# Starting block 1's loop over groups during block 0's last periods, in SBUF that earlier stages have left

## The chip, the core and the metric

The kernel runs on one core of one Trainium2 chip. A core has five engines that run side by side: TensorE (matrix products), VectorE, ScalarE, GpSimd, and SyncE, which here only starts transfers. Each engine takes its instructions in order. The metric is device microseconds of one execution. The median before the change is 1409.62 us over three runs (1408.16 to 1410.97).

## What is computed

Two blocks work on 8192 tokens (32 sequences of 256) of width 128, all in float32. Cut to what matters here:

```python
# block 0
xn = layernorm(x)
s  = attention_and_mlp(xn)            # two layers: norm, softmax attention, norm, MLP of 512
m0 = routed0(xn) + shared0(xn)        # 64 experts, each takes the first 64 tokens that chose it
x  = x + s * silu(m0)
# block 1
xn = layernorm(x)
s  = linear_attention(xn)             # keys and values twice, product of states, norm
top = argmax(xn @ gate_w)             # one of 32 experts for each token
xs  = xn * sigmoid(max(xn @ gate_w))
g  = silu(shared1(xn) + expert[top](xs))
out = x + s * g
```

For block 1 the tokens are sorted by expert: a token's place is the start of its expert plus its rank, the number of earlier tokens that chose the same expert.

## The kernel before, in words

The tokens form 64 tiles of 128, and 16 groups of four tiles; two groups are a pair. The Tile framework decides the order of each engine's queue when the program is built: it follows the order of the calls, lets a later instruction pass one that it takes to be waiting, and adds the semaphore waits. A tile comes from a pool, under a tag with a number of buffers ("bufs"); a new tile waits until the old one in its buffer is no longer used. Pools that are closed give their SBUF to later pools, with the same kind of wait.

**Block 0** (L135 to L594) runs in 18 periods, the loop over `k` at the end of its scope. `order_of` lists 16 units, each a pair and a layer. Period k interleaves, step by step, the softmax of unit k (`softmax`, L393), the second norm, MLP and projections of its neighbours (`beside`, L539), the choice of block 0's experts (`front`, `search`, `share`, in periods 0 to 6) and two groups of four experts (`experts(q)`, L297). An expert group gathers tokens with GpSimd (L305), and adds its results into the DRAM tensors `moe0[0]` and `moe0[1]` by indirect DMA (L343). They run in periods 8 to 15. Periods 16 and 17 hold only the end of the MLP: `narrow` (L496, matmuls L500) reads weights that lie in the pool w0.

**Block 1** begins behind that. Its pools w1 and wk1 are opened when block 0's are closed, so they lie where block 0's were. Each group g passes `route(g)` and then `shared1(g)`:

1. L635 to L642: load the two parts of m0 (tiles c_g and c_m), add them on GpSimd (L638), load x, apply silu on ScalarE, multiply by s_rows (which is s) and add to x, both on VectorE.
2. `normed` (L104): statistics on VectorE (L110, L111), the root by a power on GpSimd (L112, L113), and with `on_act=False` the scaling of four tiles on GpSimd (L121) into c_xn.
3. Four transpositions on TensorE (L128), a copy by ScalarE (L648).
4. The router's matmuls (L652), maximum and index on VectorE (L660, L661), the one-hot `hot` (L664), the score (L666).
5. s_rows is set to xn times the score (L670, ScalarE). GpSimd adds up `before`, the counts of earlier tiles (L673, L678), TensorE turns them into ranks (L676, L677), and VectorE stores `rank` (L681).
6. to 8. The shared expert: two halves (L690 to L693) and the second product (L698), stored by L704.

`rolling(steps, 2)` (L719) starts a new group after every second round over the groups that are under way, one step of each a round. Each of these steps ends at a `yield`, and a group's end is a step too, so that 16 groups make 144.

When all ranks are known, the places `dest` follow (L738 to L768), then 64 indirect DMAs send the rows to `xslot` (`send`, L774), `linear_attention` (L787) runs for 15 groups beside it, `routed` (L863) runs the experts in 24 lots of four tiles, and `finish` (L915) writes the output.

Of the kernel before, what the change touches and what calls it, by code (L numbers as in the profile page):

```python
# [25 lines left out]
P = 128  # L26
# [3 lines left out]
GT = 4  # L30
# [30 lines left out]
def recurrent_kernel(ctx: ExitStack, tc: tile.TileContext, x, consts, small0, wsd, wgu, wd, small1, bias1, wr, out):  # L61
# [35 lines left out]
    zero = keep.tile([P, GT * (D + 1)], F32, name="zero")  # L97
    pool.memset(zero, 0.0)
# [5 lines left out]
    def normed(wk, src, dst, on_act=False):  # L104
# [9 lines left out]
        if on_act:  # L114
            ins = pool.tensor_tensor(rs[:, 1], mv[:, :, 0], rs[:, 0], ALU.mult)
            for j in range(GT):
                vec.tensor_scalar(dst[:, j], src[:, j], rs[:, 0, j : j + 1], rs[:, 1, j : j + 1], ALU.mult, ALU.subtract)
            return ins
        pool.tensor_scalar(rs[:, 1], mv[:, :, 0], -1.0, 0.0, ALU.mult, ALU.add)
        for j in range(GT):  # L120
            ins = pool.tensor_scalar(dst[:, j], src[:, j], rs[:, 1, j : j + 1], rs[:, 0, j : j + 1], ALU.add, ALU.mult)  # L121
# [12 lines left out]

    with ExitStack() as c0:  # L135
        w0 = c0.enter_context(tc.tile_pool(name="w0", bufs=1))
        wk = c0.enter_context(tc.tile_pool(name="wk0", bufs=2))
# [4 lines left out]
        def fetch(g):  # L142
            xi = wk.tile([P, GT, D], F32, name="x_in", bufs=3)
            sp.dma_start(xi, rows(x, g))
            return xi
# [34 lines left out]
        iot = w0.tile([P, GW], F32, name="iot")  # L180
        for h in range(2):
            pool.iota(iot[h * E0 : (h + 1) * E0], [[-1, GW]], base=T - h * GW, channel_multiplier=0, allow_small_or_imprecise_dtypes=True)
        ciota = w0.tile([E0, C0], F32, name="ciota")
        pool.iota(ciota, [[1, C0]], base=0, channel_multiplier=0, allow_small_or_imprecise_dtypes=True)
        cand = w0.tile([P, NG // 4, C0], F32, name="cand")
        keys, lent, found = {}, {}, []

        def enter(g):
# [7 lines left out]
            xt = wk.tile([P, GW], F32, name="xs", bufs=5)  # L196
# [4 lines left out]
        def choose(p):  # L201

            sel = wk.tile([P, GT, 2, E0], F32, name="sel")
            for h in range(2):
# [6 lines left out]
                nm = wk.tile([P, GT], F32, name="r_nm")  # L211
                vec.tensor_reduce(nm, lg3, AX.X, ALU.max, negate=True)
                ex = wk.tile([P, GT, E0], F32, name="r_ex")
                rep = wk.tile([P, GT, E0], F32, name="r_rep")
                m8 = wk.tile([P, GT, K0], F32, name="r_m8")
# [7 lines left out]
                su = wk.tile([P, GT], F32, name="r_su")  # L223
# [4 lines left out]
                wt = wk.tile([P, GT, E0], F32, name="r_wt")  # L228
# [7 lines left out]
            if p % 2 == 0:  # L236
                keys[p // 2] = wk.tile([P, 2 * GW], F32, name="key", bufs=2)
# [35 lines left out]
        def places():  # L273
            top = w0.tile([P, C0], F32, name="top")
            yield from largest(top, cand.rearrange("p q c -> p (q c)"))
            both = w0.tile([E0, 2 * C0], F32, name="both")
# [4 lines left out]
            first = w0.tile([E0, C0], F32, name="first")  # L281
            yield from largest(first, both)

            slot = w0.tile([E0, 2, C0], F32, name="slot")
# [83 lines left out]
        def project(g, l, got):  # L368
# [6 lines left out]
            for i, rot in enumerate(("rotq", "rotk")):  # L375
                ps = bank()
                pe.matmul(ps, w[i], xt, start=True, stop=True)
                t = wk.tile([P, GW], F32, name=f"a_qk{i}", bufs=4)
# [9 lines left out]
            v = wk.tile([P, GT, D], F32, name="a_v", bufs=4)  # L388
# [4 lines left out]
        def softmax(gs, l, qkv, early):  # L393
# [3 lines left out]
            def scores(g, b):  # L397
# [11 lines left out]
                nm = wk.tile([P, 4], F32, name="a_nm", bufs=4)  # L409
# [4 lines left out]
            def exp(g, b, sc, nm):  # L414
                pr = wk.tile([P, 4, SEQ], F32, name="a_pr", bufs=3)
                su = wk.tile([P, 4], F32, name="a_su", bufs=4)
# [15 lines left out]
            def turn(g, b, pr):  # L432
                pt = wk.tile([P, 2, HEADS, SEQ], F32, name="a_pt", bufs=2)
# [7 lines left out]
            def mix(g, b, pt):  # L441
# [8 lines left out]
                if b == 0:  # L450
                    at[g] = wk.tile([P, GW], F32, name="a_at")
# [136 lines left out]

        for k in range(units + 2):
            steps = [beside(k), front(k), search(k), share(k)]  # L590
            steps += [experts(q) for q in range(E0 // 4) if min(8 + q // 2, 15) == k]
            if k < units:
                gs, l = unit(k)
                steps = [softmax(gs, l, qkv, k < 7), *steps]  # L594
            drain(run(*steps))
# [4 lines left out]
    s1, n_s1 = columns(SMALL1)  # L600
    sw1 = w1p.tile([P, n_s1], F32, name="sw1")
    sp.dma_start(sw1, small1)
    bias = w1p.tile([P, 5 * D], F32, name="bias1")
    sp.dma_start(bias, bias1.broadcast_to([P, 5 * D]))

    def par1(name, at=0, n=None):
        a, b = s1[name]
        return sw1[:, a + at : b if n is None else a + at + n]

# [4 lines left out]

    xt_all = w1p.tile([P, T], F32, name="xt_all")
    x_all = w1p.tile([P, NT, D], F32, name="x_all")
    hot = w1p.tile([P, NT, E1], F32, name="hot")
    rank = w1p.tile([P, NT], F32, name="rank")
    before = w1p.tile([P, GT + 1, E1], F32, name="before")
    vec.memset(before, 0.0)  # L620
    ones = w1p.tile([P, P], F32, name="ones")
    vec.memset(ones, 1.0)
    eiota = w1p.tile([P, E1], F32, name="eiota")
    pool.iota(eiota, [[1, E1]], base=0, channel_multiplier=0, allow_small_or_imprecise_dtypes=True)
# [6 lines left out]
    def route(g):  # L631

        tl = slice(g * GT, (g + 1) * GT)
        gr = wk.tile([P, GT, D], F32, tag="gate", name="c_g", bufs=3)
        sp.dma_start(gr, rows(moe0[0], g))  # L635
        more = wk.tile([P, GT, D], F32, tag="chan", name="c_m", bufs=3)
        sp.dma_start(more, rows(moe0[1], g))
        pool.tensor_tensor(gr, gr, more, ALU.add)  # L638
        sp.dma_start(x_all[:, tl], rows(x, g))
        act.activation(gr, gr, AF.Silu)  # L640
        vec.tensor_tensor(gr, gr, s_all[:, tl], ALU.mult)
        vec.tensor_tensor(x_all[:, tl], x_all[:, tl], gr, ALU.add)  # L642
        yield
        xn = wk.tile([P, GT, D], F32, tag="tok", name="c_xn", bufs=3)
        normed(wk, x_all[:, tl], xn)
        yield
        ps = transposed(xn)
        act.copy(xt_all[:, g * GW : (g + 1) * GW], ps)  # L648
        yield
        lp = bank()  # L650
        for j in range(GT):
            pe.matmul(  # L652
                lp[:, j * E1 : (j + 1) * E1], xt_all[:, (g * GT + j) * P : (g * GT + j + 1) * P], par1("router"),
                start=True, stop=True,
            )
        lg = lp[:, : GT * E1].rearrange("p (t e) -> p t e", e=E1)
        m8 = wk.tile([P, GT, 8], F32, name="c_m8")
        i8 = wk.tile([P, GT, 8], U32, name="c_i8")
        for j in range(GT):
            vec.max(m8[:, j], lg[:, j])  # L660
            vec.max_index(i8[:, j], m8[:, j], lg[:, j])  # L661
        fi = wk.tile([P, GT], F32, name="c_fi")
        vec.tensor_copy(fi, i8[:, :, 0])
        vec.tensor_tensor(hot[:, tl], bcast(eiota, 1, GT), bcast(fi, 2, E1), ALU.is_equal)  # L664
        score = wk.tile([P, GT], F32, name="c_sc")
        act.activation(score, m8[:, :, 0], AF.Tanh, scale=0.5)  # L666
        yield
        vec.tensor_scalar(score, score, 0.5, 0.5, ALU.mult, ALU.add)
        for j in range(GT):
            act.activation(s_all[:, g * GT + j], xn[:, j], AF.Copy, scale=score[:, j : j + 1])  # L670

        for j in range(GT):
            pool.tensor_tensor(before[:, j + 1], before[:, j], hot[:, g * GT + j], ALU.add)  # L673
        ps = bank()
        ranks = ps[:, : GT * E1]
# [39 lines left out]
    def drain(i):  # L715
        for _ in i:
            pass
# [313 lines left out]
```

## Time and profile before

| | us |
|---|---|
| Median of three runs | 1409.62 |
| The profiled execution, its own time | 1416.91 |
| Its span, first to last instruction | 1415.1 |
| TensorE busy | 1245.2 (88%) |
| VectorE busy | 926.6 (65%) |
| ScalarE busy | 771.6 (55%) |
| GpSimd busy | 703.4 (50%) |
| Mean granted TensorE clock | 0.953 |

All times in the trace count from the start of the span. Block 0 ends at 808 us, the loop over groups at 984, the sends at about 1105. An engine is called busy while one of its instructions runs; matmuls overlap, so a group of them is shorter than the sum of its durations. DVE is VectorE, ACT ScalarE, POOL GpSimd, PE TensorE and PEld its weight loads. The granted clock is the share of full speed at which TensorE ran. A line such as "A <- B" in a list of waits says that A's engine stood idle until B was done.

### The profile page before, as it was taken

The numbers are of one execution on the slowest core, as the hardware profiler recorded it, in microseconds if no ns is written. First come the engines' busy times: TensorE is split into PE (matmuls) and PEld (weight loads), VectorE is DVE, ScalarE is ACT, GpSimd is POOL, SyncE is SP. The second block draws the span as 40 slices with busy tenths as digits, with TensorE's granted clock in tenths as the row PEclk, the third lists the DMA queues.
The fourth block names the chain that finished last, engine by engine and source line by source line (L and its number), as shares of the span: only waits on it lengthen the run. The fifth ranks groups of instructions, "written<-read, shape, count | busy, mean of one in ns | idle before, by whom it ended". The sixth has DMA issues, their size and how long they took to land. (4 is left out here: it accounts for less than half of the span.)

```text
span 1415.1 us, 22851 instructions
## 1 busy us (share of the span) xinstructions
PE 1245.2 (88%) x7395; PEld 872.8 (62%) x7395; DVE 926.6 (65%) x2971; ACT 771.6 (55%) x1842; POOL 703.4 (50%) x1116
## 2 busy tenths in 40 slices
PE   6988998899899999999999758899756899899897
PEld 4545665665567666776666525566434778787763
DVE  4689899869956676566655355746555565665437
ACT  1775566566756766766757333443423454555342
POOL 6353437352356666676574176642566444343440
PEclk9989999999999999999999968999778899999999
DMA  6021332310202212222211174211411466666666
GB/s 185 9 56 54 108 110 70 106 34 5 90 13 47 47 26 40 53 52 45 45 18 9 35 215 127 58 38 38 123 53 51 129 189 203 191 191 203 185 199 195
DMA packets 141783, 128.95 MB, mean 91 GB/s; under 512 B 17792, under 2 KB 117088, under 8 KB 141536
## 3 DMA queue, kind: packets, MB, share of 16 engines
q1 hardware_dynamic: 129888, 111.72, 26.8%
q0 software_dynamic: 11776, 15.78, 4.9%
q8 instruction: 59, 0.97, 0.3%
q14 instruction: 60, 0.49, 0.1%
HBM read 85.20 MB, written 42.25 MB: 90 GB/s over the span
## 5 line engine op out<-in xcount | busy, mean ns | idle before, releaser
L904 POOL DMA_INDIRECT back<-e_ys,e_toi x96 | 97.1, 1011 | 137.7 <-ACT e_ys L903 108.0
L420 ACT ACTIVATE a_pr<-ps_sc,a_nm 128x256 f32<-128x256 f32 x256 | 119.4, 479 | 74.6 <-DVE a_nm L411 63.7
L112 POOL TENSOR_SCALAR bn_rs<-bn_mv 128x4 f32<-128x4 f32 x112 | 26.9, 241 | 243.6 <-DVE bn_mv L111 228.7
L482 PE MATMUL ps_mm<-xt,sw 128*128 128x512 f32 x256 | 132.8, 622 | 2.8 <-ACT r_ex L217 2.0
L121 POOL TENSOR_SCALAR z<-s_rows,bn_rs 128x128 f32<-128x128 f32 x256 | 129.4, 517 | 6.9
L500 PE MATMUL ps_mm<-sw,m_h 128*128 128x128 f32 x1024 | 128.0, 281 | 2.7 <-ACT a_at L452 1.3
L500 PEld LDWEIGHTS ps_mm<-sw,m_h 128*128 128x128 f32 x1024 | 120.1, 194 | 15.3 <-issue 5.6
L343 POOL DMA_INDIRECT moe<-e_y,sidx x64 | 93.2, 1456 | 59.7 <-ACT e_y L339 44.1
L487 DVE SCALAR_TENSOR_TENSOR m_h<-m_h,m_z 128x512 f32<-128x512 f32 x128 | 89.1, 702 | 48.9 <-ACT m_h L486 48.3
L113 POOL TENSOR_TENSOR bn_rs<-bn_rs,power 128x4 f32<-128x4 f32 x112 | 114.7, 1024 | 1.3
L484 ACT ACTIVATE m_z<-ps_mm,fold 128x512 f32<-128x512 f32 x128 | 86.8, 687 | 43.4 <-PE ps_mm L482 43.2
L411 DVE TENSOR_REDUCE a_nm<-ps_sc 128x2 f32<-128x512 f32 x128 | 83.1, 682 | 31.4 <-PE ps_sc L405 29.3
L890 PE MATMUL ps_sc<-e_xt,e_w 128*128 128x128 f32 x768 | 100.5, 278 | 3.3 <-ACT e_xt L877 2.4
L890 PEld LDWEIGHTS ps_sc<-e_xt,e_w 128*128 128x128 f32 x768 | 93.8, 194 | 9.6 <-issue 5.6
L405 PE MATMUL ps_sc<-a_qk,a_qk 64*128 64x256 f32 x512 | 95.4, 412 | 1.4 <-ACT a_pr L420 1.2
L486 ACT ACTIVATE m_h<-m_z 128x512 f32<-128x512 f32 x128 | 80.3, 636 | 1.8
L437 PEld LDWEIGHTS ps_tr<-con,a_pr 128*128 128x128 f32 x512 | 58.8, 144 | 32.2 <-issue 20.3
L774 POOL DMA_INDIRECT xslot<-s_rows,dest x64 | 64.1, 1002 | 27.9 <-issue 17.9
L437 PE MATMUL ps_tr<-con,a_pr 128*128 128x128 f32 x512 | 74.6, 280 | 3.4 <-DVE key L238 2.4
L438 ACT COPY a_pt<-ps_tr 128x512 f32<-128x512 f32 x128 | 70.4, 590 | 10.1 <-PE ps_tr L437 8.9
L899 PE MATMUL ps_mm<-e_w,e_hs 128*128 128x128 f32 x384 | 61.7, 288 | 15.1 <-DVE e_hs L896 11.1
L446 PE MATMUL ps_mm<-a_pt,a_v 128*64 128x256 f32 x512 | 71.5, 398 | 3.5 <-ACT r_ex L217 2.2
(226 smaller groups left out, 2956.6 us busy)
## 6 DMA issues: line engine op xcount, KB each, us to landing
e_w<-in_wr_dram SPq DMA_DIRECT2D x96, 384.0 KB
xslot<-zero SPq DMA_DIRECT2D x4, 1548.0 KB
e_x<-xslot SPq DMA_DIRECT2D x24, 258.0 KB
e_wg<-in_wgu_dram SPq DMA_DIRECT2D x16, 384.0 KB
x_in<-in_x_dram SPq DMA_DIRECT2D x16, 256.0 KB
tab<-s_rows SPq DMA_DIRECT2D x16, 256.0 KB
moe<-s_y SPq DMA_DIRECT2D x16, 256.0 KB
moe<-zero SPq DMA_DIRECT2D x4, 1024.0 KB
```

The source lines that it names most:

```text
L113: pool.tensor_tensor(rs[:, 0], rs[:, 0], power, ALU.pow)
L121: ins = pool.tensor_scalar(dst[:, j], src[:, j], rs[:, 1, j : j + 1], rs[:, 0, j : j + 1], ALU.add, ALU.mult)
L343: pool.indirect_dma_start(out=moe0[e % 2], out_offset=bass.IndirectOffsetOnAxis(ap=sidx[:, 4 * q + e : 4 * q + e + 1], axis=0), in_=ye[:, ...
L405: pe.matmul(sc[h][:, j * SEQ : (j + 1) * SEQ], qk[0][hd, q0 : q0 + P], qk[1][hd, b * SEQ : (b + 1) * SEQ], start=True, stop=True,)
L420: act.activation(pr[:, n], sc[h][:, j * SEQ : (j + 1) * SEQ], AF.Exp, bias=nm[:, n : n + 1], accum_out=su[:, n : n + 1],)
L437: pe.transpose(pts[:, n * P : (n + 1) * P], pr[:, n, k * P : (k + 1) * P], ident)
L482: pe.matmul(ps, par("w1", l * FF0 + f * P, P), xt, start=True, stop=True)
L484: act.activation(z, ps, AF.Identity, bias=fold[:, l, 3 + f : 4 + f])
L487: vec.scalar_tensor_tensor(h, h, 1.0, z, ALU.add, ALU.mult)
L500: pe.matmul(ps[:, j * D : (j + 1) * D], hs[f][:, j * P : (j + 1) * P], par("w2", l * FF0 + f * D, D), start=f == 0, stop=f == 3,)
L890: pe.matmul(ps[:, c * P : (c + 1) * P], wt[:, c * P : (c + 1) * P], xt[:, j * P : (j + 1) * P], start=True, stop=True,)
L904: ins = pool.indirect_dma_start(out=back, out_offset=bass.IndirectOffsetOnAxis(ap=toi[:, j : j + 1], axis=0), in_=ys[:, j], in_offset=None,)
```

## The change

- Block 1's helpers (`route`, `shared1`, `rolling`, `begin`) are defined ahead of block 0. The iterator `begun` over the loop's steps is made ahead of the periods; 12, 30 and 20 of its steps are taken in periods 15, 16 and 17, and the rest is drained where the loop stood.
- Block 0's pools move to the other end of SBUF. Those of the token choice (wf) close before period 7, and those of attention (wa) before period 16. In the room that they leave, the pools first_work and first are opened before period 7 (groups 0 to 3, one buffer for each tag), and mid_work and mid before period 16 (groups 4 to 8, two buffers). Groups 9 to 15 keep their tiles in w1.
- x_all, xt_all and hot are split into tiles for each group or quarter. Where three buffers of a tag rotated, `work(n)` now takes first_work if n % 3 is 0, and mid_work otherwise; linear attention, the experts and `finish` use these too.
- Groups 0 to 7 use tanh for silu: silu(x) = 0.5 (1 + tanh(x/2)) x.
- Block 1's norm scales on ScalarE, and s_rows is scaled on GpSimd.
- GpSimd no longer counts. VectorE adds up the four tiles of a group (`c_cum`), TensorE makes of them the ranks and the group's count, and `before` holds a count for each group. The counts are then added in the dest stage by quarters.
- Block 0's experts run in periods 7 to 14.
- The weights small1 are loaded in two parts: router and shared expert (sw_c) in period 7, the rest (sw_a) at the old place.

```diff
-    def normed(wk, src, dst, on_act=False):
+    def normed(wk, src, dst, on=pool):
...
         pool.tensor_scalar(rs[:, 1], mv[:, :, 0], -1.0, 0.0, ALU.mult, ALU.add)
+        if on is act:
+            pool.tensor_tensor(rs[:, 1], rs[:, 1], rs[:, 0], ALU.mult)
+            for j in range(GT):
+                ins = act.activation(dst[:, j], src[:, j], AF.Identity, scale=rs[:, 0, j : j + 1], bias=rs[:, 1, j : j + 1])
+            return ins
...
+    EARLY, TANH = 4, 8
...
+    def room(pool_, gs):
+        for g in gs:
+            x_at[g] = pool_.tile([P, GT, D], F32, name=f"x_{g}")
+            xt_at[g] = pool_.tile([P, GW], F32, name=f"xt_{g}")
+            if g % 4 == 0:
+                hots[g // 4] = pool_.tile([P, NT // 4, E1], F32, name=f"hot_{g // 4}")
...
+    def work(n):
+
+        return works[len(works) > 1 and n % 3 > 0]
+
+    def route(g):
+
+        wk = works[0] if g < EARLY else work(g)
...
+        if g < TANH:
+
+            act.activation(more, gr, AF.Tanh, scale=0.5)
+            vec.scalar_tensor_tensor(gr, more, 1.0, gr, ALU.add, ALU.mult)
+            vec.scalar_tensor_tensor(gr, gr, 0.5, s_all[:, tl], ALU.mult, ALU.mult)
+        else:
+            act.activation(gr, gr, AF.Silu)
+            vec.tensor_tensor(gr, gr, s_all[:, tl], ALU.mult)
...
+        normed(wk, x_at[g], xn, act)
...
+        for j in range(GT):
+            pool.tensor_scalar(s_all[:, g * GT + j], xn[:, j], score[:, j : j + 1], 0.0, ALU.mult, ALU.add)
...
+        cum = wk.tile([P, GT, E1], F32, name="c_cum")
+        vec.tensor_copy(cum[:, 0], hot[:, 0])
+        for j in range(1, GT):
+            vec.tensor_tensor(cum[:, j], cum[:, j - 1], hot[:, j], ALU.add)
+        ps = bank()
+        pe.matmul(ps[:, : GT * E1], const("tri"), hot.rearrange("p t e -> p (t e)"), start=True, stop=False)
+        pe.matmul(
+            ps[:, E1 : GT * E1], at1["ones"], cum[:, : GT - 1].rearrange("p t e -> p (t e)"), start=False, stop=True,
+        )
+        pe.matmul(ps[:, GT * E1 : (GT + 1) * E1], at1["ones"], cum[:, GT - 1], start=True, stop=True)
+        vec.tensor_tensor(at1["before"][:, g + 1], at1["before"][:, g], ps[:, GT * E1 : (GT + 1) * E1], ALU.add)
...
+        begun = rolling([begin(g) for g in range(NG)], 2)
         for k in range(units + 2):
+            if k == 7:
+                cf.close()
+                works.append(ctx.enter_context(tc.tile_pool(name="first_work", bufs=1)))
+                begin1(ctx.enter_context(tc.tile_pool(name="first", bufs=1)))
+            if k == 16:
+                ca.close()
+                works.append(ctx.enter_context(tc.tile_pool(name="mid_work", bufs=2)))
+                room(ctx.enter_context(tc.tile_pool(name="mid", bufs=1)), range(EARLY, 9))
             steps = [beside(k), front(k), search(k), share(k)]
-            steps += [experts(q) for q in range(E0 // 4) if min(8 + q // 2, 15) == k]
+            steps += [experts(q) for q in range(E0 // 4) if 7 + q // 2 == k]
             if k < units:
                 gs, l = unit(k)
                 steps = [softmax(gs, l, qkv, k < 7), *steps]
+            more = {15: 12, 16: 30, 17: 20}.get(k)
+            if more:
+                steps.append(some(begun, more))
             drain(run(*steps))
...
-    drain(rolling([begin(g) for g in range(NG)], 2))
+    drain(begun)
...
-        vec.tensor_tensor(hot[:, tq], hot[:, tq], bcast(padf, 1, NT // nq), ALU.mult)
+        gq = slice(q * NG // nq, (q + 1) * NG // nq)
+        vec.tensor_tensor(before[:, gq], before[:, gq], bcast(padf, 1, NG // nq), ALU.add)
+        hq = hots[q].rearrange("p (g t) e -> p g t e", t=GT)
+        for j in range(GT):
+            vec.tensor_tensor(hq[:, :, j], hq[:, :, j], before[:, gq], ALU.mult)
```

## The prediction

> **What bounds the kernel now.** I read the page first (its 40 slices of 35.4 us), then busy time by stretch, then the waits and the chain inside the stretch that the change touches. Rows 2 of the page, TensorE's busy tenths and its granted clock:
>
> ```profile
> PE   6988998899899999999999758899756899899897
> ...
> PEclk9989999999999999999999968999778899999999
> ```
>
> TensorE is full from slice 6 to slice 22, falls to 7 and 5 just after it, recovers by slice 26 and dips again at 28. The first dip is the start of block 1's loop over groups. The windows (start:end, length, then busy us and instructions of PE, PEld, DVE, ACT, POOL; granted clock, DMA share, GB/s) give it numbers:
>
> ```profile
> 713.00:772.00 59.00, 56.13 (x364) 37.84 (x364) 35.16 (x100) 38.34 (x98) 38.56 (x50) 1.00 0.12 12
> 772.00:800.00 28.00, 25.00 (x113) 14.83 (x110) 11.25 (x23) 16.01 (x28) 3.80 (x8) 0.94 0.00 1
> 800.00:808.60 8.60, 7.33 (x64) 6.95 (x62) 2.77 (x4) 2.37 (x4) 0.42 (x3) 1.00 0.00 0
> 808.60:905.00 96.40, 62.34 (x248) 41.05 (x249) 55.12 (x249) 31.26 (x72) 64.47 (x117) 0.77 0.55 154
> 905.00:984.00 79.00, 74.90 (x407) 50.68 (x406) 44.49 (x230) 37.08 (x92) 32.73 (x93) 1.00 0.12 35
> 984.00:1106.00 122.00, 81.52 (x325) 54.75 (x323) 71.81 (x190) 44.80 (x50) 71.27 (x79) 0.76 0.24 73
> ```
>
> The first three rows are block 0's periods 15, 16 and 17; the fourth is the loop's ramp, the fifth its steady part. In periods 15 to 17 TensorE is the bound while the others are at 30 to 65%; in the ramp nothing is full. The chain of waits says why:
>
> ```profile
> 800.89 6.75 PE ps_mm L500 x58
> ...
> 811.38 7.54 DMA c_m<-moe
> 819.06 1.79 POOL c_g L638
> ...
> 825.07 0.97 POOL bn_rs L113
> 826.15 1.77 POOL c_xn L121 x4
> ...
> 941.88 1.79 PE ps_mm L698 x16
> ...
> 949.50 1.79 PE ps_mm L698 x16
> ```
>
> Nothing of block 1 begins before block 0's last matmul, because its tiles lie where block 0's lay. Then a load (7.5 us) and a chain over four engines come before the first transposition at 826.7. Later the chain repeats every 7.6 us (941.88 to 949.50), ending in L698: the steady pace of a group. The waits in 808 to 990 (total us, times, longest):
>
> ```profile
> PEld ps_tr L128 <- POOL c_xn L121: 30.0, 18, 19.2
> ...
> PEld ps_mm L676 <- POOL before L673: 21.5, 15, 5.3
> ...
> PEld ps_mm L652 <- ACT xt_all L648: 2.2, 1, 2.2
> ```
>
> One wait of 19 us, then many of 0.6 to 1.5 us on GpSimd: 64.5 of 96.4 us busy there.
>
> **TensorE's work, counted at full clock.** I add what TensorE must do from 713 (start of period 15) to 984 (the loop's end), 271 us.
> - Block 0: 56.13 + 25.00 + 7.33 = 88.5 us, less 1.4 us that were only a slower clock (780 to 790, granted 0.78 and 0.88): 87.1. At period 15's own fill (56.13/59 = 95%) this takes 91.6.
> - The loop: 16 groups at 7.6 us = 121.6. Check: busy times the clock over 5 us windows gives 50.9 for the ramp, plus 74.9, less about 5 of linear attention (L809) that already ran before 984: 121.
> - Of 271 us, 271 - 213.2 = 58 therefore go to idle, to the clock and to waits.
>
> Weighing the clock: the Trainium skill (TensorE: Matmul & The Clock Gate, section What's actually happening) says that the clock halves after an idle window of about 3.4 us and is whole again after one busy window. The loop has one such long gap, so by the rule 3.4 x 0.5 = 1.7 us are lost. The windows show more: 62.3 us busy in the ramp did 50.9 us of work, 11.4 lost, with 0.50 granted still at 865 to 870 where single waits are 2 to 5 us. By the rule the gain below would be 10 us less; I take the windows.
>
> **The change, part by part.**
> - *62 of the loop's 144 steps go into periods 15 to 17* (12, 30, 20; each group has eight steps and an end). With lag 2 that is groups 0 to 5 whole, five steps of 6, three of 7: about 55 us of TensorE work by the rows (per group 0.9 L128, 1.0 L652, 0.9 ranks, 2.2 per half of the shared expert, 1.8 L698). It is added to TensorE, not hidden there; what vanishes is the ramp. After: 213.2, plus what follows.
> - *Do the other engines hold it?* Vector: 49.2 us busy now in periods 15 to 17. A tanh group is 10.7 us by durations (3 x 0.70 gate, 1.75 statistics, 1.83 max and index, 0.51, score 0.27, counts 0.95, ranks 0.57, 4 x 0.68 shared); durations overlap, busy is 0.77 of their sum in 808 to 984, so 8.2. For 6.8 groups 56: 105 of about 145 us. Scalar: 56.7 + 6.8 x 5.2 = 92. GpSimd: 42.8, less two experts' 14, plus 6.8 x 4.9 = 62. None binds. The drained rest has silu groups at 8.6 x 0.77 = 6.6 Vector us against TensorE's 7.9: nearer, not over.
> - *Counts.* GpSimd loses 4 x 0.294 + 0.273 = 1.45 us a group. Vector gains a copy, three 128x32 adds and one add from PSUM, about 0.95 (0.19 each: between a 128x8 search, 0.19, and a 128x128 product, 0.29). TensorE gains one matmul of 32 columns: 0.3 (L742's pair) to 0.5 (two of L676), I take 0.3: 4.8 us in all, less 0.3 for L742 dropped. This is on the path: **+4.5**. What it buys is the 1.43 us wait on L673 (21.5/15).
> - *Normalising on Scalar, scaling s_rows on GpSimd.* A swap: 4 x 0.474 (L121) against 4 x 0.39 (L670), with a second pointer operand 0.09 more each (L852 776 ns against L484 687). Even; nothing queued behind them is the bound.
> - *Tanh for groups 0 to 7*: Vector +0.70 for the gate and +1.38 for f_h, inside the sum above. It keeps the exponential's table: a load is 1.28 us (L640), and only one stays.
> - *Experts in 7 to 14*: gathers ran at 392.5, right after gidx (389.5), while their transpositions came at 432; starting a period earlier costs nothing visible, 0 to 2 us if period 7 waits. GpSimd idled 14 to 21 us at a time there. Its 32 loads on SP move with it. What it frees: the last scatter, now at 763, falls to about 730 (those whose place it takes ended at 723.6), so that c_g and c_m can be loaded in period 15.
> - *SP's queue*: three loads and a store per group pass into periods 15 to 17, where DMA's share is 0.00 to 0.12. sw_c (400 KB of the 786) goes in period 7. Groups 9 to 15 still need room that only block 0's end frees: their x loads start there, and then the 7.7 us from the add at 819.0 to the transposition at 826.7. By then groups 6 to 8 leave about 20 us of TensorE work. Cover nearly whole: 0 to 8, I take **+3**.
> - *Ports.* A rule speaks against the change: the Trainium skill (SBUF — State Buffer, Who interferes with whom) says that a Vector operation with two SBUF inputs and a GpSimd operation that reads SBUF block each other entirely. The gates, hot and counts are such operations, about 3.2 us a group, now beside GpSimd's z norms. The rows: z takes 517 ns mean against 442 at least, c_xn 474 against 438, so 8 to 17%. By the row 55 GpSimd operations lose 0.08 us each, 4 us in all, off the path; by the rule 6.8 x 3.2 = 22 us of blocking, of which what precedes a transposition counts. I take **+2**.
> - *New waits of TensorE in periods 15 to 17*: 26 points (transposition, router, ranks, L698, for 6.5 groups) need another engine. With softmax and the MLP to fill, 0 each at best; at worst 1.43. I take 0.1 to 0.15: **+3**.
> - *Rooms*: groups 0 to 3 work in single buffers; three rotating buffers become one plus two chosen by g % 3, for linear attention and the experts too. There "chan" is shared by two counters, so l_ot can meet a held room (four blocks of experts last 309/24 = 13 us, part of that once or twice): 0 to 6. Dest gets 4 + 1 smaller Vector operations a quarter for one of 0.68: +0.9 on the first send. Together **+2**.
>
> Sum: 213.2 + 4.5 + 3 + 2 + 3 + 2 = 227.7; before 271 (the +2 falls after 984). Gain 43. The 984 to 1106 stretch (sends, linear attention at clock 0.76) and all after it only move. The profiled execution took 1416.9 us (span 1415.1), which would become about 1374; against the median, 1409.6 - 43 = **1366.6 us**.
>
> **The rivals.**
> - *Nothing lost* (0.13): TensorE stays as full as at 700 to 720, the four allowances vanish: gain 53 to 58, about 1354. For it: three independent chains can fill each other; against: period 16's row is 25.0 of 28.
> - *The loop keeps its chain's pace* (0.20): each 1 to 2 us gap lets the clock fall as at 865 to 900 (0.50 to 0.84). Over the 73 us that are drained at 0.82, 13 us. 43 - 13 = 30 gained, from 23 to 38: about 1380.
> - *The change begins less than it says* (0.09): single rooms make groups 0 to 3 serial. xn lives from the norm to its scaling, 9 us by the rows, some 15 with queues, against 7.6. If 2.8 of the 6.8 groups slip, 2.8 x 7.4 = 21 us idle: about 1388.
> - *Slower* (0.05): TensorE's queue is in order, so a loop step that is not ready stops softmax behind it, and Scalar and Vector behind that. It decides from 43/26 = 1.65 us per point. At L652's wait of 2.2, 57 us: +14, about 1424. Against it: z's transpositions, the same pattern, wait 7.8 us over 12 in 690 to 808, 0.65.
> - Within 0.2%, which is about what a measurement of this kernel can tell: 0.03, between the last two.
>
> The main case (0.50) spans gains of 38 to 52. Range: main, nothing lost and the chain's pace hold 0.83: 1346 to 1387. Faster 0.92, same 0.03, slower 0.05.
>
> **What would show it.** Right: c_g loads before 745; the first transposition of c_xn in period 15; no TensorE slice under 8 between block 0 and the sends; granted clock 1.00 there; L698 at 7.6 to 8.2 us a group in the drained part; the last rank near 937 instead of 981; the same length from there on. Wrong: waits of TensorE on c_xn or hot over 1.5 us in periods 15 to 17; a hole at groups 9 to 11; or linear attention and the experts taking over 309 us as they do from 1106 now.

## The result and the profile after

The changed kernel takes 1385.85 us (median of 4 runs, 1384.71 to 1387.02) against 1410.3 us for the kernel before beside it: a ratio of 0.983, with a 95% interval of 0.981 to 0.985, or 24.5 us gained. I had said 1366.6 us, a gain of 43; the range held the time, its middle did not: the gain lies outside the main case (38 to 52). The profiled execution has a span of 1384.8 us (1415.1 before).

The rows of TensorE and of its granted clock in the profile after, 40 slices of 34.6 us:

```profile
PE   6988999899989999999997989899766889999898
...
PEclk9999999999989999999998999999977899999999
```

The dip to 5 at the start of the loop is gone; the one at the sends stays. A 7 stands in the 22nd slice (from 727 us), where the loop now begins. The windows of after (start:end, length, then busy us and instructions of PE, PEld, DVE, ACT, POOL; clock, DMA share, GB/s), cut at the events that cut those of before:

```profile
370.00:429.00 59.00, 49.97 (x291) 33.57 (x292) 37.68 (x137) 31.62 (x84) 32.95 (x49) 0.88 0.28 74
727.00:787.00 60.00, 49.45 (x283) 33.36 (x282) 40.80 (x137) 33.19 (x84) 31.98 (x52) 0.91 0.18 43
787.00:829.00 42.00, 38.19 (x218) 25.99 (x217) 31.34 (x113) 24.68 (x54) 20.37 (x34) 0.96 0.35 96
829.00:868.00 39.00, 37.34 (x199) 25.25 (x198) 29.69 (x107) 24.89 (x50) 16.82 (x29) 1.00 0.25 74
868.00:962.00 94.00, 86.33 (x467) 61.27 (x466) 71.08 (x354) 40.33 (x90) 36.37 (x78) 0.96 0.26 74
962.00:1077.00 115.00, 81.58 (x332) 54.57 (x330) 74.92 (x203) 47.08 (x52) 72.28 (x79) 0.81 0.25 78
```

The first row is period 7; the same stretch of the kernel before is this row of its windows:

```profile
369.00:414.50 45.50, 40.50 (x237) 26.34 (x235) 33.74 (x126) 27.25 (x70) 21.76 (x39) 0.96 0.09 28
```

Rows 2 to 4 are periods 15, 16 and 17 with early steps in them, row 5 the drained loop, row 6 sends and linear attention. A ledger of the two profiled executions by these events, with TensorE's busy time split by the clock of the records (work is busy time less what a halved clock took from it; the last three columns go from before to after):

| stretch | before, us | after, us | work | standing | lost to the clock |
|---|---|---|---|---|---|
| start to period 15 | 713 | 727 | | | |
| of that, period 7 | 45.5 | 59.0 | 38.8 to 43.4 | 5.0 to 9.0 | 1.7 to 6.6 |
| period 15 to the loop's end | 271 (713 to 984) | 235 (727 to 962) | 211.4 to 202.1 | 45.3 to 23.7 | 14.3 to 9.2 |
| sends, to the first e_x | 122 | 115 | 60.4 to 64.0 | 40.5 to 33.4 | 21.1 to 17.6 |
| the rest | 309 | 308 | | | |

So 36 us are gained where the prediction looked, 8 more behind it, and 14 are paid ahead of it, in a period that the prediction had called free: 30 us by the two spans (1415.1 to 1384.8). The 36 are not all waits that went. Standing and clock fall by 26.7 us (59.6 to 32.9); the work falls by 9.3, since two expert groups (4.6 us) now run in period 7 and some 5 us of linear attention (L809), which ran ahead of 984 before, now runs behind 962. Against the medians it is 24.5, because the profiled execution of before took 1416.9 us, 7 over its median, and that of after 1386.8, 1 over.

Where TensorE stands in the early part: the chain of waits after, from 731 us on (start, us, what):

```profile
731.46 3.64 DMA moe<-e_y,sidx
735.12 2.82 DMA c_m<-moe
738.07 1.27 POOL c_g L185
```

ScalarE's timeline at that point (start, us, line, what; in brackets its idle time ahead):

```profile
731.79 0.47 ACT L625 ACTIVATE a_at<-ps_mm,fold 128x256 f32<-128x256 f32 x1
739.37 0.63 ACT L189 ACTIVATE c_m<-c_g 128x512 f32<-128x512 f32 x1 [7.10 <-POOL c_g L185]
739.90 1.05 ACT L611 COPY a_pt<-ps_tr 128x512 f32<-128x512 f32 x2
```

The experts' last scatter lands at 735, c_g and c_m are loaded and summed, and group 0's gate (L189) waits 7.1 us for that at the head of ScalarE's queue. Behind it stands softmax's copy of a_pt, which TensorE needs: TensorE stands 6.0 us and then works at half clock until 746. This is a relative of the prediction's slower rival, at one place: there TensorE's own queue was to hold softmax, here it is ScalarE's. The four longest holes of the stretch on TensorE's timeline:

```profile
740.52 1.33 PE L610 MATMUL ps_tr<-con,a_pr 128*128 128x128 f32 x5 [6.00 <-ACT a_pt L611]
753.15 2.08 PE L633 MATMUL ps_mm<-sw,a_at 128*128 128x128 f32 x8 [2.18 <-ACT a_at L625]
812.23 1.62 PE L131 MATMUL ps_tr<-con,z 128*128 128x128 f32 x4 [3.05 <-POOL z L124]
900.61 0.77 PE L232 MATMUL ps_mm<-hot,con 128*128 128x128 f32 x2 [3.08 <-DVE hot L218]
```

The second is of the first one's make: block 0's a_at stands on ScalarE behind the loop's c_xn (L121), which waits 2.4 us for bn_rs. The third is so in part. The loop's sum of c_g and c_m waits 6.0 us at the head of GpSimd's queue, and the norm behind it, which z needs, begins about 1 us after its statistics are there (808.3, 809.3). The fourth is the loop's own chain, from the router to hot. Each of the four is followed by half clock. The pace of the drained part is not the 7.6 us of before either: the last ten ranks come 8.6 us apart in the mean (874 to 960), the last five 7.4.

### The profile page after: what moved, and what is told of

Read it like the earlier page. It is cut to its first block, busy times and chain, and to the rows that moved or that the text cites. A ratio compares the mean times of both kernels' runs of the same rounds, so it can differ in the third digit from the quotient of the medians.

```text
span 1384.8 us, 22930 instructions
## 1 busy us (share of the span) xinstructions
PE 1244.0 (90%) x7425; PEld 877.7 (63%) x7425; DVE 956.0 (69%) x3091; ACT 775.8 (56%) x1842; POOL 684.9 (49%) x1052
## 4 chain that ended last, share of the span: by engine, by line
PE 56%; DVE 18%; ACT 8%; POOL 6%; issue 6%; DMA 4%; another core or an unknown queue 1%; SPq 0%; POOLq 0%; ACTq 0%; DVEq 0%
PE ps_mm L673 6%; PE ps_mm L655 6%; PE ps_sc L578 4%; PE ps_mm L619 3%; PE ps_tr L131 3%; PE ps_tr L610 3%; PE ps_mm L550 3%; PE ps_sc L961 3%; PE ps_sc L880 3%; PE ps_mm L970 3%; DMA e_x<-xslot 2%; PE ps_tr L902 2%; PE ps_mm L560 2%; PE ps_mm L633 2%; POOL bn_rs L111 2%
## 5 line engine op out<-in xcount | busy, mean ns | idle before, releaser
L660 DVE SCALAR_TENSOR_TENSOR m_h<-m_h,m_z 128x512 f32<-128x512 f32 x128 | 89.7, 707 | 46.4 <-ACT m_h L659 45.3
```

## The experiments

The chips of the experiments run the kernel before in 1396 to 1405 us, so each kernel is given by its ratio to the kernel before on its own chip. The edits are to the changed kernel. The further columns are times in each kernel's own profile: the end of the thirteenth of the 16 pairs of narrow sums into s_rows, where period 15 begins (13th sum); the last of these sums; the first and last rank; and the issue of the last send.

| kernel | median us | ratio (95%) | 13th sum | block 0's end | first rank | last rank | last send |
|---|---|---|---|---|---|---|---|
| before, its own profile | 1410 | 1 | 717 | 808 | 842 | 981 | 1104 |
| e7_control: the change | 1370.4 | 0.981 (0.979 to 0.984) | 730 | 867 | 780 | 958 | 1064 |
| e11_tanh5 | 1370.3 | 0.981 (0.979 to 0.984) | 731 | 868 | 781 | 957 | 1063 |
| e5_norm_back | 1372.1 | 0.982 (0.980 to 0.985) | 729 | 872 | 783 | 960 | 1066 |
| e10_experts15_begin16 | 1371.9 | 0.983 (0.981 to 0.984) | 717 | 864 | 807 | 961 | 1067 |
| e2_begin16 | 1377.8 | 0.986 (0.983 to 0.988) | 732 | 870 | 817 | 968 | 1072 |
| e3_tanh3 | 1380.3 | 0.987 (0.985 to 0.990) | 733 | 879 | 786 | 973 | 1079 |
| e9_experts15 | 1379.6 | 0.988 (0.986 to 0.989) | 720 | 878 | 774 | 968 | 1074 |
| e12_held | 1388.2 | 0.988 (0.985 to 0.991) | 719 | 875 | 800 | 967 | 1076 |
| e4_no_early | 1380.8 | 0.988 (0.985 to 0.991) | 733 | 836 | 848 | 972 | 1076 |
| e13_gate_later | 1382.9 | 0.991 (0.990 to 0.993) | 734 | 883 | 789 | 974 | 1080 |
| e1_experts8 | 1382.8 | 0.991 (0.989 to 0.994) | 742 | 878 | 792 | 970 | 1074 |
| e8_rooms_alone | 1386.9 | 0.993 (0.991 to 0.995) | 733 | 842 | 848 | 977 | 1082 |

### The change again

> The changed kernel itself, once more, so that the other kernels have it beside them: the kernel before took 1395.9 us beside the first four experiments and 1410.3 us beside the changed kernel. If the ratio holds (0.983): 1372 us. Then the early start alone is worth 9 us (the kernel without it took 1380.8 us). If the changed kernel gains as many us fewer as the kernel before is quicker here (its slack being in the stages that are quicker): 1380 to 1386 us, and the early start alone is worth nothing to the end, though its last rank comes 12 us earlier (960 against 972 us).

It took 1370.4 us: the first of the two cases, the ratio holds. From the last rank to the last send it takes 106 us here and 114 in the profile after (960 to 1074); all kernels of the experiments take 104 to 110, so this is probably the chip's. Ahead of the last rank the two profiles agree to 2 us.

### What the early start is worth

e4_no_early:

```
-            more = {15: 12, 16: 30, 17: 20}.get(k)
+            more = None
```

with TANH set to 0.

> The changed kernel with no step of block 1's loop beside block 0 (the loop starts when block 0 is done; all gates by silu; rooms, experts in 7 to 14, normed on ScalarE and counts on Vector are kept). It prices the early start alone. Theory: the ramp of the first groups and the loop's pace return, so the loop ends later by what the early start brought, 25 to 40 us over the changed kernel, 1411 to 1426 us: with the 7.6 us of period 7 still paid this is as long as the kernel before or longer. Rival (most of the gain is from the moved normed, scale and counts, not from the start): under 10 us over the changed kernel, below 1396 us.

Neither: it is 10 us over the control, at the edge of what I gave the rival (and not for the rival's reason, as the next kernel shows), and 15 us under the kernel before. The control's last rank comes 14 us earlier (972 to 958), and its time is 9 or 10 us less. Not all of that need be the early steps': with every gate by silu, ScalarE loads tables three times among the softmax of periods 15 and 16 (at 734, 764 and 774), where the control does so once, at 829. What this costs was not tested apart. The reason that so little is lost is that the loop is not held to block 0's end by its place in the text. The order on an engine is made by the builder, and with the rooms free it draws the loop forward by itself. ScalarE's timeline of e4_no_early, which has no early step:

```profile
733.98 0.47 ACT L625 ACTIVATE a_at<-ps_mm,fold 128x256 f32<-128x256 f32 x1
734.47 1.28 ACT L193 ACT_TABLE_LOAD   x1
741.62 0.63 ACT L193 ACTIVATE c_g<-c_g 128x512 f32<-128x512 f32 x1 [5.87 <-POOL c_g L185]
742.16 1.05 ACT L611 COPY a_pt<-ps_tr 128x512 f32<-128x512 f32 x2
```

Group 0's gate stands at 741, the first transposition of c_xn at 803, both ahead of block 0's end at 836. Its first rank comes 12 us after that end, where it was 34 us in the kernel before. So most of the ramp goes without the listed steps, and these only move TensorE's share of the loop further forward. The same hole behind the gate is there as well (6.1 us).

### The rooms, without the swaps of engines

e8_rooms_alone is e4_no_early with normed(wk, x_at[g], xn) on GpSimd, the scaling of s_rows on ScalarE, and the copy and the three sums of c_cum on GpSimd.

> The changed kernel without the early start (no step of the loop beside block 0, gates by silu), and also with the norms back on GpSimd, the scaling of s_rows back on ScalarE and the running sum of the counts on GpSimd: of the change the rooms and the experts' periods are left. Without the early start alone, the trace shows block 0 ending at 836, the first rank at 848 and the last at 972 us: 12 us of ramp (34 before) and 8.3 us a group (9.3 before). Theory A (the swaps of engines set the loop's pace, the rooms the ramp): the pace goes back to 9.3 us, 14 to 16 us over the kernel without the early start, 1394 to 1397 us. Theory B (the ramp and the pace were both those of rooms that came free late): no more than 4 us over it, 1381 to 1385 us.

It is 6 us over e4_no_early by the medians (0.5% by the ratios, 0.993 against 0.988, with intervals that only just meet), with the last rank at 977 against 972: between the two theories. The ramp is 6 us here without the swaps, so theory B has the ramp. The pace from first to last rank is 8.6 us a group against 8.3, so of the engines' swaps some 5 us remain, a third of theory A.

e5_norm_back undoes the norm and the scale with the early start kept:

> The changed kernel with the norms of the loop back on GpSimd and the scaling of s_rows back on ScalarE; the early start is kept. GpSimd gets four operations on 128 columns a group for the norm (0.45 us each, some 1.8 us) and loses four for the scale (0.40 us each); ScalarE the reverse. Theory (ScalarE's norm holds softmax's copies behind its wait for bn_rs, and the early steps' stalls come from ScalarE's queue): 2 to 6 us under the changed kernel. Rival (the loop's drained part needs the norm on ScalarE, since GpSimd has the c_g sums, pow and scale before it): 2 to 8 us over it. No change within 2 us if neither binds.

It took 1372.1 us against 1370.4, with intervals that overlap: the swap is even, as predicted. The 5 us of e8_rooms_alone are then either those of the running sum on GpSimd or of swaps that matter only in a loop without early steps; the runs don't part the two.

### Where the loop begins, and where the experts stand

e2_begin16:

```
-            more = {15: 12, 16: 30, 17: 20}.get(k)
+            more = {16: 36, 17: 26}.get(k)
```

> The changed kernel with block 1's loop begun in period 16, not 15 (no steps in 15, 36 in place of 30 in 16, 26 in place of 20 in 17). In the trace after, TensorE stands for 6.0 us at 734.5 because the copy of a_pt on ScalarE is queued behind the first group's tanh gate, which waits for c_g and c_m, and the clock is 0.50 from 739.4 to 746.2 (3.4 us more). Theory: if that stall is a pure loss it goes with the early step, worth up to 9 us, but the groups' first loads come some 25 to 45 us later and the same wait for loads stands at the head of period 16, with fewer softmax steps behind it; net 0 to 6 us less than the changed kernel, 1380 to 1386 us. Rival (the start in period 15 carries the gain: the later start brings the ramp back): 5 to 15 us more, 1391 to 1401 us.

1377.8 us against 1370.4, 7 us slower: the rival. And the hole was not removed: the waits of TensorE's weight loads in 730 to 800 list 6.9 us on the a_pt copy again, since the builder puts the gate at 741 here too.

e1_experts8 gives the experts three, two, two, three, two, two and two groups in periods 8 to 14:

```
-            steps += [experts(q) for q in range(E0 // 4) if 7 + q // 2 == k]
+            qs = [q for q in range(E0 // 4) if 8 + 7 * q // 16 == k]
+            steps += [lane(qs[0::2]), lane(qs[1::2])]
```

> The changed kernel with the experts put in periods 8 to 14 (in two lanes) in place of 7 to 14; all else kept. In the trace after, period 7 became 13.1 us longer, of which 5.5 us is the two expert groups' TensorE work, which is taken out of period 15 anyway, and some 7.6 us is stall (gaps of 3.3, 2.1 and 2.8 us on TensorE between 387 and 416 us) with the granted clock at 0.5 after them. Theory: these stalls belong to the experts' standing beside the places of token choice, so without them period 7 is as long as before and the time falls by 5 to 8 us under the changed kernel, to 1378 to 1381 us. Rival (the work is only moved and the stall follows it to period 8 or later): 1384 to 1387 us, no change.

Both miss; it is 12 us over the control. Period 7 ends as before (at 415, against 414.5), but each of the two periods with three groups is 12 us longer (458 to 513, 600 to 656, where two groups take 43). It comes to period 15 12 us later than the control and stays 12 us late to the last rank.

e9_experts15 puts them back where they were:

```
-            steps += [experts(q) for q in range(E0 // 4) if 7 + q // 2 == k]
+            steps += [experts(q) for q in range(E0 // 4) if 8 + q // 2 == k]
```

Its early groups read the rows of moe0 ahead of the last experts' sums, so they are computed without these: its time is that of a kernel that leaves this wait out.

> The changed kernel with the experts in periods 8 to 15 as before; all else kept. In the traces, period 7 is 13 to 15 us longer with two expert groups in it, periods 8 to 14 (two expert groups each) are as long as before, and period 15 of the kernel without the early start (no experts in it) is as long as the one of before (48 and 46 us between its first and last narrow sums). Theory: the experts in period 15 were free, and in period 7 they cost 13 us, so undoing this move gives 8 to 13 us, less what they take from the loop's early steps in period 15 (up to 5.5 us of TensorE work): 4 to 12 us under the changed kernel. Rival: period 15 with the loop's steps and the experts both is too full, and gives the 13 us back: within 3 us of the changed kernel, or over it.

The rival: it is 9 us over the control. Period 15 begins 10 us earlier (720), and more than that is lost again behind it: TensorE stands 10.0 us at 724, for the a_pt copy behind group 0's gate as before, and from the 13th sum to block 0's end it takes 158 us where the control takes 137.

e10_experts15_begin16 joins e9's line with e2's, and so reads no row too early:

> The changed kernel with the experts in periods 8 to 15 as before and the loop begun in period 16 (36 steps, and 26 in 17), so that no row is read ahead of the experts' sums. Known: beginning in 16 with the experts in 7 to 14 took 1377.8 us against 1370.4; with the experts in 8 to 15, period 7 was 10 us shorter (narrow sums at 418, not 428 us). Theory (the two add up): 1377.8 less 10, 1366 to 1370 us. Rival (the experts' last sums come some 30 us later, at 753 us as before, and the first groups' loads wait for them, so that the loop has no work for period 16): 1376 to 1386 us, the 10 us given back.

1371.9 us: no different from the changed kernel, and between the two cases. The windows of e10_experts15_begin16 (columns as above): period 7, period 15, then to block 0's end and to the last rank:

```profile
369.00:415.00 46.00, 41.41 (x239) 26.80 (x235) 33.91 (x127) 27.21 (x70) 21.61 (x40) 0.96 0.19 58
...
717.00:768.00 51.00, 47.50 (x310) 32.05 (x308) 28.63 (x79) 31.48 (x84) 32.02 (x41) 1.00 0.13 16
768.00:864.00 96.00, 77.87 (x372) 51.23 (x372) 66.23 (x253) 52.49 (x104) 46.88 (x74) 0.89 0.33 95
864.00:961.00 97.00, 90.70 (x482) 63.47 (x481) 73.81 (x357) 43.39 (x95) 40.79 (x86) 0.96 0.24 71
```

Those of the control:

```profile
372.00:428.00 56.00, 45.95 (x283) 31.18 (x279) 36.93 (x135) 30.94 (x81) 32.87 (x49) 0.94 0.28 73
...
730.00:785.00 55.00, 44.04 (x258) 29.11 (x257) 38.41 (x131) 32.88 (x85) 29.54 (x50) 0.94 0.17 45
785.00:867.00 82.00, 76.17 (x414) 51.70 (x413) 61.37 (x218) 49.35 (x102) 37.23 (x63) 0.96 0.30 84
867.00:958.00 91.00, 83.14 (x445) 58.39 (x445) 68.63 (x339) 39.58 (x88) 35.73 (x78) 0.96 0.27 75
```

The experts in period 15 cost nothing there (51 us at full clock), and period 7 keeps its 46 us: 13 us in hand at the 13th sum. Then the loop, begun in 16, meets 18 us of standing and a clock of 0.89 before block 0's end, where the control's row of 82 us has 6 us and 0.96. By the last rank the two are 3 us apart. The move of the experts is the price of a start in period 15, and the start is worth just about that price.

Period 7's holes are seen on TensorE's timeline of after; the second and third are the experts':

```profile
390.27 0.25 PE L463 MATMUL ps_mm<-con,slot 64*128 64x64 f32 x1 [3.31 <-DVE bn_mv L109]
...
397.95 0.44 PE L485 MATMUL ps_tr<-con,e_gx 128*128 128x128 f32 x1 [2.10 <-DMA e_gx<-tab,gidx]
...
418.88 1.55 PE L619 MATMUL ps_mm<-a_pt,a_v 128*64 128x256 f32 x6 [2.85 <-ACT e_y L512]
```

In e10_experts15_begin16 the first stays at 3.31 us, as it is in the kernel before (3.28), and the other two are gone.

### The gate out of softmax's way

e13_gate_later, the list turned holding the copies of a_pt as they are written:

```
+            g or tc.add_manual_dep(ins.ins, turned[-1].ins.name, order, reason="the gate goes after the turn")
```

> The changed kernel with one order added: the tanh gate of the first group stands in ScalarE's queue behind the last copy of a_pt that is written ahead of it, not in front of it; all else kept. In the control the gate waits 6.9 us at the head of ScalarE's queue for the GpSimd sum of c_g and c_m (738.8), and TensorE stands 5.8 us for the a_pt copy behind it (734.1 to 739.9). Theory (one gate out of place holds softmax, a pure loss): the gap goes, block 0's end and the loop's end come 5 to 9 us earlier, 1361 to 1366 us against 1370.4. Rival (the stall is taken over by what waits next, since the first group then comes later and period 15 is waiting on softmax anyway): within 2 us of the changed kernel.

It is 12.5 us slower than the changed kernel: worse than either theory. The gate comes at 742.5 with no idle time ahead of it and the 5.8 us hole is gone, but the next step of the same group brings one. TensorE's timeline of e13_gate_later:

```profile
755.65 1.99 PE L550 MATMUL ps_mm<-xt,sw 128*128 128x512 f32 x4 [0.38 <-ACT m_z L657]
762.00 1.24 PE L131 MATMUL ps_tr<-con,c_xn 128*128 128x128 f32 x3 [4.37 <-ACT c_xn L121]
```

Group 0's transposition stands in front of period 16's projections (L550) and waits for its norm. That is 4.4 of the 12.5 us; the order of all that follows differs too (block 0 ends at 883, not 867), so one place was not changed alone, and where the rest goes is open. That the hole is a pure loss is not borne out.

e12_held keeps the experts in 8 to 15 and holds the early steps until the last of them is written out:

```
+        def held(steps):
+            while len(done) < E0 // 4:
+                yield
+            yield from steps
...
+                steps.append(held(some(begun, more)))
```

> The experts in periods 8 to 15 as before, and the loop's 12 early steps of period 15 held until the last expert group of that period is written out, 30 and 20 steps in 16 and 17 as in the changed kernel; all else is the changed kernel. Known beside the kernel before at 1396 us: the changed kernel 1370.4 us; experts in 8 to 15 with the loop from period 16 on 1371.9 us (its first rank 807 us against 780, its last 961 against 958). Theory (what is lost by beginning in 16 is the 27 us by which the first rank comes later, of which half can be had back after the experts' last sums, while period 7 stays short): 1365 to 1369 us. Rival (the loop's end is set by TensorE's work and by waits that turn up wherever the loop begins, some 35 to 40 us of standing and low clock from period 15 to the last rank in every kernel so far): 1370 to 1374 us, no better than the changed kernel.

0.988, worse than both. The waits of e12_held in 764 to 785 (who waited for whom: total us, times, longest):

```profile
PEld ps_tr L131 <- ACT c_xn L121: 14.2, 2, 14.0
PE ps_tr L131 <- ACT c_xn L121: 13.6, 1, 13.6
...
ACT c_m L189 <- POOL c_g L185: 6.6, 1, 6.6
```

The last scatter is issued at 766, and the load of c_m follows at 769; group 0's chain (load, sum, gate, add, norm) is ready at 780. Its transposition stands at the head of TensorE's queue from 766 on and holds block 0 for 13.6 us. This is the prediction's slower rival as it was written.

### Is Vector the bound of the drained part?

e3_tanh3 and e11_tanh5 set TANH, 8 in the change, to 3 and to 5.

> The changed kernel with the gates of groups 3 to 7 by silu in place of tanh: three Vector operations on 512 columns fewer in each of five groups (some 2 us of Vector a group), and a table load on ScalarE where silu follows the last exponential. In the trace after, Vector is at 100% from 875 to 895 us and the loop goes at its pace. Theory (Vector binds the drained loop): 3 to 8 us less than the changed kernel, 1378 to 1383 us, and the TensorE gaps between 868 and 905 us shrink. Rival (TensorE's order binds, Vector's load only looks full): within 2 us, 1384 to 1388 us.

> The changed kernel with the gates of groups 5 to 7 by silu, where the last exponential is past (783 us, group 5's gate is after 800); three groups' worth of Vector operations on 512 columns fewer (about 2 us each). The kernel with groups 3 to 7 by silu took 1380.3 us: group 3's silu stands before an exponential, with two table loads of 1.28 us more on ScalarE, so it did not test Vector. Theory (Vector is what binds between 868 and 905 us, where it was 100% busy): 3 to 5 us under the changed kernel, 1365 to 1367 us. Rival (what binds there is the chain of each group and TensorE's order, Vector's load fills its waits): within 2 us, 1368 to 1372 us.

e3_tanh3 took 10 us more: a Silu of group 3 comes before the last exponential, and ScalarE loads tables three times (1.28 us each) between 780 and 880, where the control does so once. That this is the whole of the 10 us was not tested. e11_tanh5 is the clean one. Its window of the drained part:

```profile
868.00:957.00 89.00, 82.48 (x454) 57.50 (x453) 67.28 (x335) 40.11 (x89) 35.91 (x78) 1.00 0.28 77
```

From 785 to the last rank Vector is busy 125 us against 130 in the control, in 870 to 895 it is busy 19.6 us against 22.6 in the profile after, and the time is the same. Vector's full slices there fill waits; they don't set the pace (in three windows of 5 us after, Vector is busy 5.00).

## Why the prediction was right in sign and 18 us off

- *TensorE bounds the stretch, and the ramp goes.* Right. The first load of c_g is at 732.5 ("before 745"), the first transposition of c_xn in period 15, and standing falls by 21.6 us, the clock's loss by 5.1. Before, 59.6 of 271 us were standing or clock. Of the signs named, no slice is under 8 between block 0 and the sends, but the clock there is 0.96 and not 1.00, and the last rank comes at 960, not near 937.
- *TensorE's work.* The sum had 213.2 + 4.5 for the counts; it was 202.1, and 206.7 with the 4.6 us of the two expert groups that went to period 7. So 11 us were to the good. Of these 4.5 are no work: the sum carried them as standing inside block 0's 91.6 us (87.1 at a fill of 95%). The counts' matmuls came as said by their durations: 19.5 us for three kinds after, 14.7 before.
- *The step that failed: the allowances for new waits, rooms, ports and the x loads, 3 + 2 + 2 + 3 = 10 us.* What is left of standing and clock in the stretch measured 32.9 (23.7 and 9.2); with the 4.5 inside block 0's term the prediction had 14.5. I had put 0.1 to 0.15 us on each of 26 points in periods 15 to 17. There standing and clock are 22.2 us of 141 after and 8.8 of 95.6 before, so 13.4 more, or 0.5 a point; the prediction would have had it slower from 1.65 on. The four holes (14.3 us) and the half clock behind them (9.2) make up 23.5 of the 32.9. I had named an in-order queue that holds block 0 behind a loop step that isn't ready as the slower rival, and given it 0.05, because z's transpositions wait 0.65 us each. But z's chain starts from s_rows, which lies in SBUF; the loop's first group has a scatter and two loads ahead of its own. And I had looked at TensorE's queue alone, while it was ScalarE's, and once GpSimd's, that held. The row was near in kind and far in depth.
- *The rival whose number came.* A gain of 24.5 lies in the range of "the loop keeps its chain's pace" (23 to 38, 0.20). Its mechanism did not come: it had the drained part at a clock of 0.82, and the row has 0.96, with 7.7 us of standing in 94. That the range held the time is in this part luck: the misses happened to add up to what another case had.
- *Experts in 7 to 14, "nothing visible, 0 to 2 us".* Period 7 became 13.5 us longer: 4.6 of work that was moved, and 8.9 of holes and low clock. e10_experts15_begin16 shows the 13 us back when they stand in 8 to 15. The sum did not ask what covers them: in period 7 two of the holes are the experts' own waits, for a gather to land and for e_y on ScalarE; in period 15 they cost nothing in that kernel.
- *"All after it only move."* 7 us were gained from there to the sends' end. From the last rank to the first send it took 8.3 us before and 3.8 after, since the total now comes with the last group and not from L742 behind the queue of L698. I had +0.9. What makes the rest was not tested.
- *The swap of norm and scale is even.* Shown by e5_norm_back.
- *Ports, +2.* The blocking that the rule speaks of is there, and the change adds next to none of it. The z norms on GpSimd in periods 15 to 17, first before, then after (ns: least, median, most):

```profile
L121 POOL TENSOR_SCALAR z<-s_rows,bn_rs x24: 442/448/981, 725.2 to 781.7; 128x128 f32<-128x128 f32 x24
L124 POOL TENSOR_SCALAR z<-s_rows,bn_rs x24: 436/447/964, 734.5 to 813.0; 128x128 f32<-128x128 f32 x24
```

  The medians hide it. Laid beside Vector's timeline, the 10 of after that overlap a Vector operation with two inputs in SBUF take 686 ns in the mean and up to 964, the other 14 take 436 to 448; before it is 8 at 707 and 16 at 442 to 448. Over 447 ns each, that is 2.4 us after and 2.1 before. Nearly all of it is beside block 0's own m_h (L660); one z of 939 ns runs beside the loop's add to x.
- *"None binds" of the other engines.* Shown for Vector's load by e11_tanh5. By its order it did not hold: ScalarE was at 55% in period 15 and its queue stopped TensorE twice.
- *The drained pace, 7.6 to 8.2 us.* It was 8.6 over the last ten ranks.

Put together for the profiled executions: the stretch gained 36 us, not 43, being the 43 less 23 (allowances of 10 that became 33) plus 16 (work of 217.7 that became 202.1, of which 4.6 is paid in period 7). From the 36 go 14 for period 7, and 8 come from the sends and after: 30.

What the change is made of, by the ratios: the rooms, with the experts' periods and the total that comes with the groups, 0.7%; the engines' swaps and the running sum on Vector 0.5%, without the early start; the early start, together with the tanh gates that go with it, another 0.7%. Each of these is uncertain by 0.2 to 0.4%. Every arrangement measured loses some 30 us or more to standing and clock between period 15 and the last rank (32.0 in the control, 40.6 in e10_experts15_begin16, 48.3 in e8_rooms_alone; 59.6 before), at much the same work. Whether an order without these holes exists stays open: no arrangement here beats the changed kernel.

## What to carry to other kernels

When work of a next stage is begun beside the last of this one, price its first item by the whole chain that makes it ready, and ask on each in-order queue what stands behind it. A stall that is taken away at one step of that chain can come back at the next (e13_gate_later), and holding the whole chain back can stop another queue (e12_held). That a later order gains is shown by no run here: the four kernels that began or gated the loop later were level or slower. And a period that seems to have room because one engine idles there should be costed with its holes, not only with its busy time.

## What the runs showed of the hardware

TensorE's granted clock has only two values in the records of all fourteen profiles, 1.00 and 0.50, and its low stretches are mostly one (130 of 271), two (93) or three (30) times 3.4 us long. For the idle gaps of TensorE up to 960 us that began at full clock, I counted those with a low stretch that began no later than 3.4 us after the gap's end: all 20 gaps of over 4.25 us, 46 of 48 of 2.75 to 4.25 us (41 of the 48 under 3.4), 28 of 47 of 1.75 to 2.75, and 13 of 107 of about 1 us (0.9 to 1.1). The profiles share places (a gap of 3.3 us in period 7 is in all fourteen), so the cases are fewer than the counts. The Trainium skill (TensorE: Matmul & The Clock Gate, section What's actually happening) has the clock fall after an idle window of about 3.4 us in windows that run freely; here gaps of 2.75 us and more were followed by a window or two of half clock nearly every time, and gaps of 1.75 to 2.75 three times in five. A hole of 3 us is thus to be priced, as an estimate from these counts, at 3 us and some 2 more for one or two windows at half clock (1.7 to 3.4 us).

On GpSimd, a norm of 128x128 took 436 to 453 ns with no Vector operation beside it, and up to 1398 beside two Vector operations with both inputs in SBUF (m_h, L660, in the profile after).
